# Three token scatters in two steps instead of two, and a smaller share of each step for the experts

## The chip, the cores and the metric

The kernel runs on one core of a Trainium2 chip. Its engines are TensorE (PE; weight loads are listed as PEld), VectorE (DVE), ScalarE (ACT), GpSimd (POOL) and SyncE (SP), each with its own instruction stream in program order; SP, ACT and POOL also issue DMAs. The metric is the device time of one execution in microseconds; lower is better.

## The reference, cut to what matters

The input is 8 sequences of 512 tokens with 256 features, all in float32. Two layers follow one another, each of the form x + attention(norm(x)) + feed-forward(norm(x)).

- Layer 0, attention: 16 heads of 16 features over all 512 tokens of a sequence, plain softmax.
- Layer 0, feed-forward: a mixture of 8 experts. Each token goes to the expert with the largest affinity. The expert normalizes the token again, applies a 256 to 1024 layer with ReLU and a 1024 to 256 layer, and the result is weighted by the sigmoid of the affinity.
- Layer 1, attention: causal attention, a convolution over three tokens whose output serves as queries of a second causal attention with the same keys and values, and an output projection.
- Layer 1, feed-forward: two low-rank products with a GELU between them.

```
assign = jnp.argmax(x @ centroids.T, axis=1)
h = relu(_layernorm(xs, ln_g[e], ln_b[e]) @ w1[e].T + b1[e])
ye = xs + h @ w2[e].T + b2[e]          # for the tokens of expert e
x = x + _L0_attn_ref(xn, ...) + _L0_ffn_ref(xn, ...)
```

## The kernel before, in words

Everything stays in SBUF but the tokens sorted by expert. The attention of layer 0 is cut into 32 jobs: 8 sequences, 4 groups of four heads. A loop of steps t = 0 to 268 (`run`, L442) does the attention; each job has 8 steps, and its scores are computed twice. First they are computed for the row maxima: PE at L345, DVE at L362 (`Job.scores`). A step 8 or more later, `Job.shift` (L375 to L382) transposes the maxima and writes them by four small SP DMAs into a spare row of the job's queries, so that the second computation (L394, `Job.exps`) gives scores already shifted; ACT takes their exponentials (L421) from step 12 on. `Job.attend` (L434) multiplies the exponentials with the values in every second step. When a job's last product is there, `l0_done` (L901) transposes and divides it on DVE (L904 to L908) and POOL adds it to the running sum `acc` (L912).

All other work of layer 0 is filled into these steps by the class `Work`. `fill(t, per_step, most)` (L118) runs after a step's scores and before its `attend`. It holds `room`, which grows by `per_step` = `MOE_PER_STEP` units a step, is capped at twice that, and falls by the cost of each piece placed. A piece is placed as long as room is above zero. Pieces with a due time (query, key and value projections at 1.75 units each, `shift` at 0.2) are forced when due and come first when due within four steps. Otherwise the next piece is drawn from one generator, `stream` (L843): a number is a cost, and `At(t)` closes the generator until step t. The order of instructions on every engine is the order in which these calls are made; no scheduler changes it.

`stream` runs as follows:

- The strings of `FIRST`, one per step: norms, transposes, affinities. In the second of them two SP DMAs fill the two DRAM buffers `hs_d` with zeros.
- `routing` (L673): the affinities of all tokens give each token its expert and its row in a buffer sorted by expert (`pos_i`), where each expert's rows are padded to blocks of 256 tokens, and each of the 23 blocks the row of its expert's weights (`wrow_i`). Then 32 scatters (L749), one for each 128 tokens: an indirect DMA from POOL writes 128 normalized tokens to their rows of one of the two `hs_d`, alternately, and `first_sum` (L609, POOL) adds the norm to `acc`.
- The memory of the norms is released, `load_ffn` issues weight loads on SP, and `Block(moe, 0)` is made: POOL gathers the 2.2 MB of the expert's weights `w` by an indirect DMA (L764), SP loads the block's 256 rows from both `hs_d` (L773), and POOL adds the two (L778). The generator then waits five steps.
- `banks_experts` (L218) gives the PSUM banks out anew: two banks for the maxima's scores and two for the exponentials' scores, where `banks_alone` (L211) gives three each; three banks instead of one for everything else.
- 23 expert blocks. Each has four `hidden` pieces (1.75 units: L807 on PE, ReLU on ACT L818 and DVE L820), `features` of the next block (0.5 units: transposes L785, `hsT` on DVE L790, which needs `w`), and two `output` pieces (3.5 units: L828, L837 and the store to `fs_d`, L839). The next `Block` is made after the first `hidden` piece.
- `banks_alone`, and the 26 strings of `SECOND`, one per step: POOL gathers expert results back (L512), DVE adds them (L522), and the norms, statistics and transposes for the first half of layer 1 follow.

Behind the loop come the feed-forward of layer 1 and its two attentions.

Of the kernel before, what the change touches and what calls it, by code (L numbers as in the profile page):

```python
# [37 lines left out]
STEPS = (8, 6)  # L38
LEAD = (12, 12)
EARLY = 4  # L40
MOE_PER_STEP = 2.08
LAG = 7


# [108 lines left out]
def block_kernel(ctx: ExitStack, tc: tile.TileContext, x, a0_wqk, a0_bqk, a0_wv, a0_bv, cent, experts,  # L153
# [412 lines left out]
    with ExitStack() as l0:  # L566
# [38 lines left out]
        def first_sum(b, c):  # L605

            norms, n = firsts0[b, c]
            a = acc[b][:, c, :]
            nc.gpsimd.tensor_scalar(a, a, norms.rs1[:, n : n + 1], norms.nm_t[:, n : n + 1], ALU.mult, ALU.add)  # L609
# [63 lines left out]
        def routing():  # L673
# [74 lines left out]
            for t in range(NT):  # L748
                nc.gpsimd.indirect_dma_start(  # L749
                    out=hs_d[t % 2][:, :],  # L750
                    out_offset=IndirectOffsetOnAxis(ap=pos_i[:, t : t + 1], axis=0),
                    in_=h0[t // NC][:, t % NC, :],
                    in_offset=None,
                )
                first_sum(t // NC, t % NC)
                yield At(todo.t + 1)

        class Block:

# [83 lines left out]
        def stream():  # L843
# [17 lines left out]
            for t, pieces in enumerate(FIRST):  # L861
                for p in pieces.split():
                    do[p[0]](int(p[1]))
                if t == 1:
                    for h in hs_z:
                        nc.sync.dma_start(out=h, in_=zeros.unsqueeze(1).to_broadcast([P, NBLK, 2 * D]))
                yield At(t + 1)
            yield from routing()
            later.close()
            moe = later.enter_context(tc.tile_pool(name="moe", bufs=2, reuse_waits="tile"))  # L870
# [28 lines left out]
        todo = Work()  # L899
# [54 lines left out]
        todo.stream = stream()  # L954
        run(jobs, todo, 0, MOE_PER_STEP, 99)
        later.close()
# [90 lines left out]
    for i in range(2):  # L1047
        t = l1.tile([P, 2, S + 2], F32, tag=f"ctxT{i}", name=f"ctxT{i}", bufs=1)
# [232 lines left out]
```

## Time and profile before

| | us |
|---|---|
| median of 3 runs | 2091.49 (2089.46 to 2093.51) |
| the profiled execution, its own time | 2091.93 |
| its span | 2090.0 |
| PE busy | 2001.5 (96%) |
| DVE busy | 1230.1 (59%) |
| ACT busy | 867.6 (42%) |
| POOL busy | 203.4 (10%) |
| L345, scores for the maxima, PE busy | 761.0 |
| L394, scores for the exponentials, PE busy | 681.2 |
| L807 and L828, experts, PE busy | 179.6 and 170.9 |
| L749, scatters, POOL busy | 33.0 (32 of 1.03 each) |
| granted PE clock, mean | 0.982 of full |

How to read it: times in the trace are microseconds from the start of the span. A busy PE is not PE at its peak, since ends of matmuls are modelled. A row of a timeline has start, length, engine, line, operation, output and inputs, the number of instructions merged, and in brackets how long the engine had stood idle and what ended that. A row of windows has the window, its length, the busy time of each engine with its number of instructions, the granted PE clock as a share of full speed, and DMA load.

### The profile page before, as it was taken

The page shows a single profiled execution, that of the slowest core. Times are in us where ns is not written, and L with a number is a line of the kernel's source. Part 1 is how long each engine was busy: PE and PEld are TensorE (multiplying, and loading weights), DVE is VectorE, ACT ScalarE, POOL GpSimd, SP SyncE. Part 2 cuts the span into 40 slices and gives each one's busy share as a digit, 9 for nine tenths or more (in the row PEclk, how much of TensorE's full clock was granted, in tenths as well). Part 3 has the DMA queues.
Part 4 walks back from the last instruction along what each step waited for, and adds up shares of the span by engine and source line. Part 5 has one row for each costly group of instructions (what it writes and reads, how often), then busy time and mean ns, then how long its engine had stood idle before and what let it go on. Part 6 is the DMA issues. An engine that isn't in the chain of part 4 may idle for free.

```text
span 2090.0 us, 35594 instructions
## 1 busy us (share of the span) xinstructions
PE 2001.5 (96%) x13672; PEld 1013.6 (48%) x13672; DVE 1230.1 (59%) x3565; ACT 867.6 (42%) x1690; POOL 203.4 (10%) x245
## 2 busy tenths in 40 slices
PE   5899999999999999998898999999999999999998
PEld 3334555555555555542334455554555555554554
DVE  5765555555455455565425666666666666666763
ACT  4444333333333333346541444444444444444444
POOL 4361010010110100013310000000000000000000
PEclk8899999999999999999997899999999999999999
DMA  9015132222322122202000000000000000000000
GB/s 329 25 64 184 59 117 81 94 79 96 117 78 97 67 108 107 74 26 80 21 0 1 2 2 2 2 12 2 2 13 2 12 2 12 2 12 2 2 12 21
DMA packets 46058, 105.60 MB, mean 51 GB/s; under 512 B 5953, under 2 KB 33985, under 8 KB 42945
## 3 DMA queue, kind: packets, MB, share of 16 engines
q0 software_dynamic: 6384, 59.78, 7.7%
q1 hardware_dynamic: 38656, 42.62, 6.1%
q8 instruction: 107, 1.75, 0.4%
q10 hardware_dynamic: 848, 0.93, 0.1%
q14 instruction: 63, 0.51, 0.1%
HBM read 76.05 MB, written 26.48 MB: 49 GB/s over the span
## 4 chain that ended last, share of the span: by engine, by line
PE 87%; DVE 6%; ACT 2%; issue 2%; DMA 1%; SPq 0%; POOL 0%; ACTq 0%; DVEq 0%; POOLq 0%
PE bank L345 30%; PE bank L434 13%; PE bank L828 8%; PE bank L807 8%; PE bank L293 5%; PE bank L412 4%; PE bank L1085 4%; PE bank L394 3%; PE bank L303 3%; PE bank L1103 2%; DVE m L362 2%; PE bank L990 1%; PE bank L1137 1%; PE bank L266 1%; PE bank L1003 1%
## 5 line engine op out<-in xcount | busy, mean ns | idle before, releaser
L421 ACT ACTIVATE e<-bank 128x512 f32<-128x512 f32 (+1 forms) x1280 | 639.1, 552 | 919.5 <-PE bank L394 460.4
L345 PE MATMUL bank<-k,q 32*128 32x512 f32 (+3 forms) x3072 | 761.0, 534 | 22.2 <-DVE m L362 18.3
L394 PE MATMUL bank<-q,k 32*128 32x512 f32 (+3 forms) x3072 | 681.2, 533 | 4.5 <-DMA q<-mT 3.4
L365 DVE CUSTOM_DVE_ANT_0 jk<-bank,cmask 128x512 bf16<-128x512 f32 (+3 forms) x1024 | 502.9, 491 | 240.8 <-PE bank L345 162.4
L345 PEld LDWEIGHTS bank<-k,q 32*128 32x128 f32 x3072 | 301.2, 186 | 384.1 <-issue 162.1
L362 DVE TENSOR_REDUCE m<-bank 128x1 f32<-128x512 f32 x512 | 328.9, 685 | 142.8 <-PE bank L394 111.8
L434 PE MATMUL bank<-e,v 128*32 128x512 f32 (+3 forms) x3072 | 317.4, 501 | 0.0
L394 PEld LDWEIGHTS bank<-q,k 32*128 32x128 f32 x3072 | 266.2, 186 | 15.0 <-issue 9.6
L807 PE MATMUL bank<-hsT,w 128*128 128x256 f32 x736 | 179.6, 389 | 1.3 <-DVE hsT L790 1.3
L828 PE MATMUL bank<-w,hT 128*128 128x256 f32 x736 | 170.9, 386 | 0.0
L807 PEld LDWEIGHTS bank<-hsT,w 128*128 128x128 f32 x736 | 133.3, 190 | 69.9 <-issue 52.8
L828 PEld LDWEIGHTS bank<-w,hT 128*128 128x128 f32 x736 | 137.4, 191 | 38.1 <-issue 21.0
L434 PEld LDWEIGHTS bank<-e,v 128*32 128x32 f32 x3072 | 67.5, 108 | 137.1 <-issue 132.0
L412 PE MATMUL bank<-mask_t,ident_bf 128*128 128x128 bf16 (+1 forms) x768 | 123.5, 244 | 0.0
L412 PEld LDWEIGHTS <-ident_bf 128*128 128x128 bf16 x768 | 44.0, 97 | 155.5 <-issue 140.5
L820 DVE TENSOR_SCALAR hT<-bank,w 128x256 f32<-128x256 f32 x92 | 44.5, 484 | 110.3 <-ACT hT L818 110.3
L1085 PE MATMUL bank<-ctxT,cw_sb 128*128 128x256 f32 x384 | 90.0, 383 | 2.1 <-DVE q L283 1.8
L365 DVE DVE_READ_ACCUMULATOR2_ANT m<- 128x1 f32 x1024 | 85.0, 83 | 0.0
L837 DVE TENSOR_TENSOR f<-bank,w 128x256 f32<-128x256 f32 x46 | 19.5, 425 | 104.2 <-PE bank L828 104.1
L285 ACT ACTIVATE k<-bank,bqk,rows 128x512 f32<-128x512 f32 x64 | 46.3, 773 | 73.8 <-PE bank L293 64.5
L818 ACT ACTIVATE hT<-bank,w 128x256 f32<-128x256 f32 x92 | 43.6, 474 | 79.8 <-PE bank L807 79.8
L1085 PEld LDWEIGHTS bank<-ctxT,cw_sb 128*128 128x128 f32 x384 | 70.1, 189 | 13.2 <-DVE q L283 3.2
(187 smaller groups left out, 1410.5 us busy)
## 6 DMA issues: line engine op xcount, KB each, us to landing
hs_d<-zeros SPq DMA_DIRECT2D x2, 5888.0 KB
hs<-hs_d SPq DMA_DIRECT2D x46, 256.0 KB
q<-mT SPq DMA_DIRECT2D x384, 2.0 KB
fs_d<-f SPq DMA_DIRECT2D x23, 256.0 KB
acc<-in_x SPq DMA_DIRECT2D x8, 512.0 KB
out<-acc SPq DMA_DIRECT2D x8, 512.0 KB
cw_sb<-in_conv_w SPq DMA_DIRECT2D x1, 768.0 KB
wqk<-in_a_wqk ACTq DMA_DIRECT2D x1, 512.0 KB
```

Of the source, the lines that this page charges most:

```text
L293: nc.tensor.matmul(ps, lhsT=w[:, k, col : col + P], rhs=src[:, k, :], start=(k == 0), stop=(k == 1))
L303: nc.tensor.matmul(ps[:, j * D : (j + 1) * D], lhsT=src[:, k, c * P : (c + 1) * P], rhs=w[:, k, :], start=(k == 0), stop=(k == 1),)
L345: lambda h=h, qc=qc, at=at, nk=nk: nc.tensor.matmul(heads[h % 2][:, at : at + nk], lhsT=self.q[h * PH : (h + 1) * PH, qc * P : (qc + 1) * ...
L362: nc.vector.tensor_reduce(self.m[:, qc, h, :], src, AX.X, ALU.max, negate=True)
L365: nc.vector.tensor_tensor_reduce(out=junk[:, :nk], in0=src, in1=cmask[:, S - nk :], scale=1.0, scalar=-3e38, op0=ALU.add, op1=ALU.max, acc ...
L394: lambda h=h, kc=kc, at=at, lo=lo: nc.tensor.matmul(heads[h % 2][:, at : at + S - lo], lhsT=self.k[h * PH : (h + 1) * PH, kc * P : (kc + 1 ...
L412: nc.tensor.matmul(heads[h][:, : len(blocks) * P], lhsT=ident_bf, rhs=mask_t[:, : len(blocks) * P], start=False, stop=True,)
L421: nc.scalar.activation(e[:, h, :], heads[h][:, :n], AF.Exp, scale=self.scale)
L434: nc.tensor.matmul(self.av[h * PH : (h + 1) * PH, lo:], lhsT=self.v[:, kc, 4 * self.g + h, :], rhs=es[h // 2][:, h % 2, :], start=first, s ...
L807: nc.tensor.matmul(ps[:, i * TB : (i + 1) * TB], lhsT=w[:, O_W1 + k * FF + fc * P : O_W1 + k * FF + (fc + 1) * P], rhs=self.hsT[:, k, :], ...
L828: nc.tensor.matmul(ps[:, 0:D], lhsT=self.hT[:, fc, j * P : (j + 1) * P], rhs=w[:, O_W2 + fc * D : O_W2 + (fc + 1) * D], start=(fc == 0), s ...
L1085: nc.tensor.matmul(ps[:, :w], lhsT=cw_sb[:, k, tap, c * P : (c + 1) * P], rhs=ctxT[b % 2][:, k, tap + lo : tap + lo + w], start=(k == 0 an ...
```

## The change

Two things are changed. The scatter loop of `routing` no longer closes the generator after each scatter: after the scatters t = 1, 4, 7, ..., 31 it goes on at once. Of 32 closings 11 go, so that steps take one, two, one, two, ... scatters and everything behind them in the generator comes eleven steps earlier in the program. `MOE_PER_STEP` falls from 2.08 to 1.97 units. The instructions themselves are the same, in another order.

```diff
@@ -38,7 +38,7 @@
-MOE_PER_STEP = 2.08
+MOE_PER_STEP = 1.97
@@ -753,7 +753,8 @@
                 first_sum(t // NC, t % NC)
-                yield At(todo.t + 1)
+                if t % 3 != 1:
+                    yield At(todo.t + 1)
```

## The prediction

> **What bounds the kernel now.** I read the page first: TensorE is busy nearly everywhere, so the change can only pay where PE has holes.
>
> ```profile
> PE 2001.5 (96%) x13672; PEld 1013.6 (48%) x13672; DVE 1230.1 (59%) x3565; ACT 867.6 (42%) x1690; POOL 203.4 (10%) x245
> ```
>
> Then I read ScalarE's timeline, because the first of a step's exponentials (L421) marks each step t of the layer-0 loop: two exponentials per step, the first pair belonging to t = 12. So step 40 starts at 146.25 us, step 51 at 173.45, step 244 at 931.25. The loop before the experts (steps 46 to 48 here) and among them (steps 81 to 84) looks like this:
>
> ```profile
> 163.42 1.08 ACT L421 ACTIVATE e<-bank 128x512 f32<-128x512 f32 x2 [1.35 <-PE bank L394]
> 165.52 1.09 ACT L421 ACTIVATE e<-bank 128x512 f32<-128x512 f32 x2 [1.02 <-PE bank L394]
> 167.38 1.08 ACT L421 ACTIVATE e<-bank 128x512 f32<-128x512 f32 x2 [0.78 <-PE bank L394]
> ...
> 295.48 1.09 ACT L421 ACTIVATE e<-bank 128x512 f32<-128x512 f32 x2 [4.63 <-PE bank L394]
> 300.21 1.08 ACT L421 ACTIVATE e<-bank 128x512 f32<-128x512 f32 x2 [3.65 <-PE bank L394]
> 302.67 1.09 ACT L421 ACTIVATE e<-bank 128x512 f32<-128x512 f32 x2 [1.37 <-PE bank L394]
> 305.70 0.60 ACT L421 ACTIVATE e<-bank 128x512 f32<-128x512 f32 x1 [0.66 <-PE bank L394]
> ```
>
> A step without filling takes 2.10 (even) or 1.86 us (odd) while three banks serve the scores; once banks_experts leaves two, it takes 2.46 (300.21 to 302.67). A step with filling is PE's sum: about 1.27 us odd, 2.26 even (with the eight attend matmuls), plus 1.73 us per 1.75 units. An empty odd step thus wastes 1.2 us of PE, an empty even one 0.2.
>
> Third, GpSimd's timeline: a scatter (L749) with its first_sum (L609) takes 1.79 us from start to start and nothing paces it in between but the attention sum of a finished job (L912), for which POOL stood idle 5.86, 6.12 and 6.12 us at steps 28, 36 and 44.
>
> ```profile
> 133.84 0.55 POOL L609 TENSOR_SCALAR acc<-acc,rs1e,nme 128x256 f32<-128x256 f32 x1
> 140.52 0.72 POOL L912 TENSOR_TENSOR acc<-acc,og 128x256 f32<-128x256 f32 x1 [6.12 <-DVE og L908]
> 141.39 1.03 POOL L749 DMA_INDIRECT hs_d<-h,pos_i  x1 [0.15 <-issue]
> 142.47 0.55 POOL L609 TENSOR_SCALAR acc<-acc,rs1e,nme 128x256 f32<-128x256 f32 x1
> 143.19 1.02 POOL L749 DMA_INDIRECT hs_d<-h,pos_i  x1 [0.17 <-issue]
> ...
> 162.52 1.03 POOL L749 DMA_INDIRECT hs_d<-h,pos_i  x1 [0.15 <-issue]
> ...
> 165.86 1.00 POOL L764 DMA_INDIRECT w<-in_experts,wrow_i  x1 [1.03 <-PE bank L394]
> 167.86 1.27 POOL L778 TENSOR_TENSOR hs<-hs,hs 128x512 f32<-128x512 f32 x1 [1.00 <-DMA hs<-hs_d]
> ```
>
> Last, PE at the first expert block: the last scatter starts at 162.52, the block's first matmul at 175.21, which is 12.69 us of scatter, weight gather (about 8.7 us to hsT) and transposes. PE lost only 1.27 us to it, in step 51.
>
> ```profile
> 173.28 0.66 PE L785 MATMUL bank<-ident,hs 128*128 128x128 f32 x4
> 175.21 1.10 PE L807 MATMUL bank<-hsT,w 128*128 128x256 f32 x4 [1.27 <-DVE hsT L790]
> ```
>
> **The change, part by part.** Every sum is against the profiled execution, 2091.93 us (span 2090.0); the median of the three runs is 0.44 us below it.
>
> *Where the steps fall.* The planner is a rule in the code and can be replayed. Scatters start at step 14 in both. Before, one per step: Block 0 is made at step 46, its features are in step 51 (the "+ 5"), the last expert piece in step 241, SECOND runs from 242 to 267 of 268. After: 1, 2, 1, 2, ... scatters per step, Block 0 at step 35, features at step 40, last expert piece in 243, SECOND from 244; its last piece f3 comes right behind the loop. The loop has 269 steps in both. So I compare the stretch from step 40 to step 244: before 931.25 - 146.25 = 785.0 us, the same 405.2 units of work in both.
>
> *Respreading (mostly a wash).* Steps by parity and units placed, with the median of their time before, and their number before (53 to 241) and after (42 to 243):
> even: nothing or 0.5, 2.46 us, 18 and 19; 1.75, 3.99, 46 and 50; 2.25, 4.43, 4 and 2; 3.5, 5.72, 19 and 20; 4.0, 6.11, 6 and 7; 5.25, 7.43, 1 and 3.
> odd: nothing or 0.5, 2.46, 14 and 22; 1.75, 3.00, 46 and 54; 2.25, 3.43, 3 and 0; 3.5, 4.73, 24 and 18; 4.0, 5.11, 8 and 7.
> Sums: 735.4 and 771.6, so +36.2. The rest of the stretch before: steps 40 to 52 took 39.5 us (with one projection pair on a single bank, step 43: 6.80 us) and 242, 243 took 4.1, together 43.6. After: steps 40 and 41 with 4.0 and 1.75 units, 6.11 + 3.00, plus 1.3 for the first hsT, 10.4. Gone: 33.2. Net +3.0. Then what lies over the medians: before 6.0 (1.4 for a wait on hs at step 179 over its class, near 679.3, 1.7 for a clock dip at step 190, 0.42 each time that a job's transposition lands in an empty odd step, three times; small rest). After: five such landings, 2.1, small rest 1.5, dips between 0 and 3.2, taken half: 5.2. Respreading: 3.0 - 0.8 = +2.2 us. The smaller share is what undoes the thirteen steps gained: empty odd steps grow from 14 to 22.
>
> *The scatters (the cost).* Emitting three per two steps gives POOL 12 scatters in eight steps, 12 x 1.79 + 0.87 for L912 = 22.3 us; eight such steps took 21.05 us (98.27 to 119.33, L912 to L912). So POOL, with its idle gone, becomes the pace. Scatter 3 starts at 90.84 as now; scatter 9 at 90.84 + 6 x 1.79 = 101.6; its sum and L912 end at 104.1; scatter 21 at 104.2 + 11 x 1.79 = 123.9; L912 ends at 126.4 (its input is there at 119.3, no wait); scatter 31 at 126.55 + 9 x 1.79 = 142.7 us. That is 19.8 us sooner than 162.52, while PE reaches the features 27.2 us sooner (146.25 against 173.45). The chain of 12.69 us then puts the first L807 at 155.4, 9.1 us into step 40 where it was 1.76 into step 51: a wait of 7.3 us more. PE is in order: behind the transposes stand step 40's hidden layers, its attend matmuls, and all of step 41, so exponentials and maxima wait too. Ends: the wait can be 4.5 if the weight gather starts as soon as POOL is free (1.03 us sooner) and the scatters keep 1.74, or 9.5 if further waits like the 1.76 us on a scatter's landing before 90.84 come in. I take 7.3, since every duration in it has a row.
>
> *What else moves with it.* SP: the ten loads of load_ffn and out_b (0.4 to 0.6 us each to issue) and Block 0's hs loads stand ahead of the next shift's row copies, as before; they now begin after step 33's shift, about 133, and are issued by 139, before the last scatter lands: hidden, worth at most 2 us if not. POOL: job 2's L912 (step 36) now stands behind the gather of w and the hs sum; its result has no reader before the experts end, and og's two buffers give 16 steps: nothing. Block 1's gather follows at about 150 and lands some 9 us later, its hs loads perhaps behind it, about 162; PE wants them in step 42, about 165: hidden by 2 to 3 us, and up to 3 us of new wait if that cover is gone.
>
> *The clock.* PE idles from 146.1 to 149 (hs sum) and from 150 to 155.4. What such holes do, in windows around the holes at 72.5 (3.39 us) and 961.9 (3.43 us); columns are window, its length, busy time of PE, PEld, DVE, ACT and POOL, clock:
>
> ```profile
> 71.10:74.50 3.40, 1.40 (x8) 0.33 (x2) 3.23 (x12) 1.08 (x2) 0.00 (x0) 1.00 0.00 0
> 77.90:81.30 3.40, 3.40 (x15) 0.90 (x12) 3.03 (x14) 2.19 (x4) 0.00 (x0) 0.50 0.00 0
> 81.30:84.70 3.40, 3.40 (x16) 1.28 (x9) 3.26 (x8) 0.09 (x1) 1.12 (x1) 0.50 0.01 2
> 965.40:968.80 3.40, 3.40 (x16) 0.61 (x16) 0.43 (x2) 1.51 (x3) 0.00 (x0) 0.50 0.85 269
> ```
>
> After the first hole PE worked 8.8 us at half speed, after the second 3.4. Hidden-layer matmuls are pure PE, so the loss is half of that: 1.7 to 4.4 us; I take 3.0, and 0 as the low end, since holes of 1.2 us left the clock at 1.00. The Trainium skill, "TensorE: Matmul & The Clock Gate", Part 1, says that after an idle window of about 3.4 us the clock halves and that one busy window restores it; by the rule alone the loss would be about 1.7 us and the sum 1.3 lower. The row at 77.9 to 84.7 shows two full busy windows still at half speed, so here the rule is too kind. It speaks against the change, as both do.
>
> *The end of layer 0.* SECOND two steps later, f3 behind the loop. Its norms and copies are ScalarE's: the last steps already run at 4.9 us a pair on four exponentials, four norms and a copy, the same instructions after. Against it, the last shift (mT at 961.58, queued behind eight statistics on DVE, PE idle 3.43 us for its rows) will stand behind only two. I take zero; ends -2.5 (that hole gone) and +2.5 (two norms 1.05, transposes 0.8, copy 0.6 exposed). Layer 1 is unchanged.
>
> **Sum:** +2.2 + 7.3 + 3.0 = +12.5; 2091.93 + 12.5 = 2104.4, and 0.44 less against the median: 2104 us.
>
> **Rivals.**
> *Block 0 is ready in time (not slower).* Place: L785 and L807 of block 0. If the scatters ran as fast as they are emitted, the last would start at step 35, 135.8 us, and the first L807 at 148.5, 2.2 us into step 40. Then only respreading remains, +2.2, and with the dips gone +0.6: about 2092 to 2094. It decides once the last scatter starts before about 137. For it: POOL's idle of 18 us. Against: the 1.79 us, constant in every burst.
> *The hole pulls more down.* The clock stayed at half for 20.5 us after 1139.5; that, or Block 1 late as well, adds 5 to 8 us: 2109 to 2112. Against: PE is full behind this hole, and was not there.
> *A gain after all.* The end of layer 0 gives back 2.5 and a clock dip, and the thin empty steps cost nearer 2.0 than 2.46 (30 x 0.46 = 14 us less): 2085 to 2088. Against: all 31 empty steps show 2.45 or more.
>
> **How the numbers follow.** Changes of 0.2% (4.2 us) are about what a measurement of this kernel can tell from none; its three runs spread over 4.1 us. Block 0 late, 2096 to 2108: 0.77. In time: 0.13. More pulled down: 0.06. Gain: 0.04. The low end of the late case, 4.5 + 0 + 0.6 = +5, less the runs' own 2 us, is 2095; the high end, 9.5 + 4.4 + 4 = +18, is 2110. Slower: the late case, the pulled down and a little of the in-time one, 0.85; same 0.11; faster 0.04.
>
> **What would show it.** In the changed profile: scatters at 1.79 us without idle before L912; the last one near 142.7; L785 waiting for POOL and L807 for hsT, together some 7 to 9 us idle on PE near 146 to 155; a clock of 0.50 after it; step 244 near 942; 22 empty odd steps at 2.46. I am wrong if L807 follows L785 within 2 us, if empty steps take 2.0, or if the end of layer 0 shortens by more than 3 us.

## The result and the profile after

The changed kernel is slower: 2103.86 us (median of 7 runs, 2096.19 to 2108.2) against 2089.46 (7 runs, 2088.76 to 2093.51), a ratio of 1.0064 with a 95% interval of 1.0049 to 1.0079. The forecast was 2104 us, slower. The profiled execution of the changed kernel took 2103.86 us, its span 2100.8; 10.8 us more than the span of before. Lines from L756 on stand one further down than before, so L807 is now L808.

TensorE is busy for 3 us more, in a span that is 11 us longer:

```profile
PE 2004.7 (95%) x13672; PEld 1013.6 (48%) x13672; DVE 1230.7 (59%) x3565; ACT 867.5 (41%) x1690; POOL 204.4 (10%) x245
```

GpSimd's timeline after the change. Scatters follow one another without a hole in front of L913, as the second line shows; the last one starts at 142.62 us (142.7 was forecast), and the first weight gather at 147.08.

```profile
122.90 0.55 POOL L609 TENSOR_SCALAR acc<-acc,rs1e,nme 128x256 f32<-128x256 f32 x1
123.42 0.71 POOL L913 TENSOR_TENSOR acc<-acc,og 128x256 f32<-128x256 f32 x1
124.29 1.03 POOL L749 DMA_INDIRECT hs_d<-h,pos_i  x1 [0.16 <-issue]
...
137.66 1.02 POOL L749 DMA_INDIRECT hs_d<-h,pos_i  x1 [0.96 <-DMA hs_d<-h,pos_i]
...
142.62 1.02 POOL L749 DMA_INDIRECT hs_d<-h,pos_i  x1 [0.97 <-DMA hs_d<-h,pos_i]
...
147.08 1.00 POOL L765 DMA_INDIRECT w<-in_experts,wrow_i  x1 [2.14 <-DMA hs_d<-h,pos_i]
```

TensorE's timeline at the first expert block: 3.24 us idle for POOL's sum of the token rows, 5.09 us for `hsT`. Before, it was 1.27 us in all.

```profile
150.39 1.11 PE L786 MATMUL bank<-ident,hs 128*128 128x128 f32 x4 [3.24 <-POOL hs L779]
156.59 5.63 PE L808 MATMUL bank<-hsT,w 128*128 128x256 f32 x16 [5.09 <-DVE hsT L791]
```

And `hsT` waits on VectorE for the weights:

```profile
155.94 0.99 DVE L791 TENSOR_SCALAR hsT<-bank,w 128x256 f32<-128x256 f32 x2 [8.08 <-DMA w<-in_experts,wrow_i]
```

ScalarE's timeline, whose exponentials (L421) mark the steps: step 40 starts at 147.21 and step 41 at 164.38. A step with the same 4.0 units takes 6.11 us elsewhere; this one takes 17.17.

```profile
147.21 1.08 ACT L421 ACTIVATE e<-bank 128x512 f32<-128x512 f32 x2 [0.78 <-PE bank L394]
160.38 0.47 ACT L819 ACTIVATE hT<-bank,w 128x256 f32<-128x256 f32 x1 [12.08 <-PE bank L808]
...
164.38 1.09 ACT L421 ACTIVATE e<-bank 128x512 f32<-128x512 f32 x2 [1.66 <-PE bank L394]
```

Windows over that hole (window, length, busy time of PE, PEld, DVE, ACT, POOL, granted clock, DMA share, GB/s): the clock is at 0.53 and 0.50 behind the first idle stretch.

```profile
146.00:150.00 4.00, 1.15 (x7) 0.31 (x6) 1.85 (x3) 1.52 (x3) 1.93 (x2) 1.00 0.57 140
150.00:154.00 4.00, 1.11 (x4) 0.71 (x4) 0.00 (x0) 0.00 (x0) 1.99 (x3) 0.53 0.96 401
154.00:158.00 4.00, 1.41 (x3) 1.18 (x4) 0.99 (x2) 0.00 (x0) 0.00 (x0) 0.50 0.96 403
158.00:162.00 4.00, 4.00 (x14) 3.16 (x12) 0.48 (x1) 0.47 (x1) 0.00 (x0) 0.69 0.91 369
```

By stage, in us between the first exponentials of the steps named. Two profiles of each kernel; the second ones are runs told of below.

| stage | before | before, again | after | after, again |
|---|---|---|---|---|
| start to step 40 | 146.3 | 146.6 | 147.2 | 145.2 |
| step 40 alone | 2.1 | 2.1 | 17.2 | 18.7 |
| steps 40 to 244 | 785.0 | 785.2 | 799.4 | 802.4 |
| steps 244 to 266, the end of layer 0 | 52.6 | 62.4 | 49.2 | 59.0 |
| step 266 to the end | 1106.1 | 1109.1 | 1105.0 | 1111.6 |

The loss is in steps 40 to 244: 14.4 us in the first pair, 17.2 in the second. The end of layer 0 varies by 10 us from one execution to another in both kernels, and is 3.4 us shorter after the change in both pairs.

### The profile page after: what moved, and what is told of

Its sections match the earlier page's. It is cut to its first block, busy times and chain, and to the rows that moved or that the text cites. A ratio compares the mean times of both kernels' runs of the same rounds, so it can differ in the third digit from the quotient of the medians.

```text
span 2100.8 us, 35592 instructions
## 1 busy us (share of the span) xinstructions
PE 2004.7 (95%) x13672; PEld 1013.6 (48%) x13672; DVE 1230.7 (59%) x3565; ACT 867.5 (41%) x1690; POOL 204.4 (10%) x245
## 4 chain that ended last, share of the span: by engine, by line
PE 85%; DVE 7%; ACT 3%; issue 2%; POOL 2%; DMA 1%; ACTq 0%; SPq 0%; DVEq 0%; POOLq 0%
PE bank L345 28%; PE bank L434 13%; PE bank L808 8%; PE bank L829 8%; PE bank L293 5%; PE bank L1086 4%; PE bank L412 4%; PE bank L394 3%; PE bank L303 2%; DVE m L362 2%; PE bank L1104 2%; PE bank L991 1%; PE bank L1138 1%; PE bank L266 1%; PE bank L1004 1%
## 5 line engine op out<-in xcount | busy, mean ns | idle before, releaser
L421 ACT ACTIVATE e<-bank 128x512 f32<-128x512 f32 (+1 forms) x1280 | 639.0, 552 | 933.9 <-PE bank L394 474.7
L808 PE MATMUL bank<-hsT,w 128*128 128x256 f32 x736 | 183.5, 394 | 5.1 <-DVE hsT L791 5.1
L808 PEld LDWEIGHTS bank<-hsT,w 128*128 128x128 f32 x736 | 135.2, 193 | 75.8 <-issue 60.3
```

Of the source, the lines that this page charges most:

```text
L421: nc.scalar.activation(e[:, h, :], heads[h][:, :n], AF.Exp, scale=self.scale)
L808: nc.tensor.matmul(ps[:, i * TB : (i + 1) * TB], lhsT=w[:, O_W1 + k * FF + fc * P : O_W1 + k * FF + (fc + 1) * P], rhs=self.hsT[:, k, :], ...
```

## The experiments

The theory on trial (A): POOL's scatters and the weight gather behind them arrive late, PE stands in step 40 and then runs cold. The rival (B): the smaller share and its empty steps are the whole loss. Each experiment is judged by its stages first, because the spread of single times, on one chip up to 14 us for the kernel before, is as large as what is sought.

**The scatters alone**

```diff
-MOE_PER_STEP = 1.97
+MOE_PER_STEP = 2.08
```

(against the changed kernel)

> The three scatters per two steps of the changed kernel with the old share of 2.08. By the planner's rule Block 0's features stay at step 40, the last expert piece comes in step 229 and SECOND runs from 230 to 255. Theory A (PE waits in step 40 for POOL's scatters and the weight gather, then runs at half clock): the wait of 8.3 us and the cold stretch stay, step 40 takes about 17 us. The steps from 40 to 256 cost some 3 us more by the table of steps, and the steps from 256 on, with no norms left in them, get shorter by up to 2.3 us a pair, six pairs: 2094 to 2104 us. Theory B (the smaller share and its empty steps are the loss, the wait is made up later): empty odd steps fall from 22 to 17, some 6 us, and the kernel comes near the one before, 2090 to 2098, with a short step 40 making no difference.

Measured: 2114.5 us, a ratio to before of 1.0081 (1.0051 to 1.0111). Both theories named a lower time; both missed. The wait is there, and its end lies where it did although PE came 3 us sooner (step 40 starts at 144.1), so POOL's chain sets it and not PE:

```profile
149.99 1.11 PE L786 MATMUL bank<-ident,hs 128*128 128x128 f32 x4 [5.91 <-POOL hs L779]
156.34 4.04 PE L808 MATMUL bank<-hsT,w 128*128 128x256 f32 x9 [5.23 <-DVE hsT L791]
```

What was mis-sized is the end. With the experts done at step 230, steps 230 to 256 took 85.4 us (909.4 to 994.8), 3.3 a step, against the 2.10 and 1.86 of unfilled steps before the experts, with the clock at half for 20.5 us in three stretches; the short pairs behind step 256 gave back 12.7 (13.1 us against 25.8 from step 256 to 266). Finishing the experts early bought nothing here.

**The share alone**

```diff
-MOE_PER_STEP = 2.08
+MOE_PER_STEP = 1.97
```

(against the kernel before)

> The smaller share, 1.97, alone; one scatter a step as before. By the rule Block 0's features are in step 51 as before, SECOND starts at 253, and its last ten strings come behind the loop. Theory A: no wait beyond the 1.3 us of before, no cold stretch, 39 empty steps against 32; the end is longer by norms without exponentials beside them but the pairs before it shorter: 2087 to 2095 us. Theory B (the share is the loss): most of the 14 us, 2098 to 2106.

Measured: 2109.91 us, 1.0066 (1.0045 to 1.0087). That is above both ranges; as a loss against before on this chip, 14.9 us, the number is B's, but the place is not. Step 266 starts 986.3 us into the span against 983.9 and 994.3 in the two profiles of before; what is lost stands behind it, 1126.1 us to the end against 1106.1 and 1109.1, where the last ten strings of SECOND now run with no attention beside them. The expectation had set them off against shorter pairs ahead of them; they cost 17 to 20 us. It also says why the share can only fall together with an earlier start.

**A scatter made cheaper for POOL**

```diff
-            nc.gpsimd.tensor_scalar(a, a, norms.rs1[:, n : n + 1], norms.nm_t[:, n : n + 1], ALU.mult, ALU.add)
+            nc.scalar.activation(a, a, AF.Identity, bias=norms.nm_t[:, n : n + 1], scale=norms.rs1[:, n : n + 1])
```

(in `first_sum`, against the changed kernel)

> The changed kernel with first_sum moved from POOL to ACT (same values, scale and bias of an Identity), so that a scatter takes POOL about 1.2 us instead of 1.79 and the order on PE is untouched. Theory A: the last scatter starts near 133 instead of 142.6, the first matmul of block 0 near 147 instead of 156.6, the wait in step 40 shrinks to at most 2 us and the clock stays up: 8 to 11 us gone, 2092 to 2096 us. Theory B (respreading is the loss): within 3 us of the changed kernel, 2101 to 2107. ACT takes 32 more instructions of some 0.53 us in steps where it is busy for half of the time.

Measured: 2105.18 us, 1.0051 (1.0033 to 1.0069). The time lies in B's range and not in A's, and the last scatter starts at 135.24 and not near 133. Step 40 fell from 17.2 to 13.9 us, not to some 8. GpSimd's timeline shows the reason: without the sum every other scatter stands idle for a landing (the two scatters after the first line below, 1.28 us and then 1.87 from start to start), so 32 of them still take 53 us. The scatters go to the two `hs_d` in turn, and each waits for the last but one, which wrote the same buffer. Behind the last scatter POOL stands idle for one of SP's loads (L876), and the gather starts 6.2 us behind that scatter instead of 4.5.

```profile
122.88 0.97 POOL L749 DMA_INDIRECT hs_d<-h,pos_i  x1 [0.92 <-DMA hs_d<-h,pos_i]
124.16 0.97 POOL L749 DMA_INDIRECT hs_d<-h,pos_i  x1 [0.30 <-issue]
126.03 0.97 POOL L749 DMA_INDIRECT hs_d<-h,pos_i  x1 [0.90 <-DMA hs_d<-h,pos_i]
...
135.24 0.97 POOL L749 DMA_INDIRECT hs_d<-h,pos_i  x1 [1.85 <-DMA hs_d<-h,pos_i]
139.01 0.75 POOL L876 TENSOR_TENSOR ob_sb<-ob_sb,fb_sb 128x256 f32<-128x256 f32 x1 [2.80 <-DMA fb_sb<-in_f_b]
141.48 0.98 POOL L765 DMA_INDIRECT w<-in_experts,wrow_i  x1 [1.73 <-PE bank L394]
```

So under POOL's 1.79 us lies a second floor, set by the landing and by having two buffers, about 1.6 us a scatter; a third buffer was not tried. The wait for the weights stays at 5.27 us, and the clock falls here too. The direction is A's, a shorter chain and a shorter step 40; steps 40 to 244 took 796.1 us, 3.3 less than in the first profile of the changed kernel.

**Ten steps ahead of the features**

```diff
-MOE_PER_STEP = 1.97
+MOE_PER_STEP = 2.0
-            yield At(todo.t + 5)
+            yield At(todo.t + 10)
```

(against the changed kernel)

> The changed kernel with ten steps instead of five between making Block 0 and its features (step 45), and a share of 2.00, so that SECOND starts at step 244 as in the changed kernel. Nothing moves off POOL. Theory A: step 45 starts near 157, when hsT can be ready, so the wait falls from 8.3 to 0 to 2 us and the clock stays up, while five more unfilled steps cost 10 us of which the experts' steps give back about the same: 2091 to 2096 us. Theory B: 2101 to 2107.

Measured: 2101.93 us, 1.0026 (1.0008 to 1.0043); that is in B's range for the time and not in A's, but the runs of before beside it had a median of 2095.01, so the time alone does not decide. By stage it is what A says: steps 40 to 244 take 786.2 us against 785.0 before and 799.4 after the change. TensorE's transposes wait for nothing, and ahead of its first expert matmul it stands idle for 1.68 us, while VectorE makes `hsT` (from 162.30 us, behind two row maxima); the weights are there by then. The step that holds the features takes 7.04 us, 1.9 over its class.

```profile
160.59 0.66 PE L786 MATMUL bank<-ident,hs 128*128 128x128 f32 x4
162.93 1.32 PE L808 MATMUL bank<-hsT,w 128*128 128x256 f32 x5 [1.68 <-issue]
```

The clock does not fall below 1.00 between 200 us and 930 us, nor around this block. The 13.2 us gained there are the wait, the cold stretch behind it and what the other spreading of the pieces (36 empty steps by the rule, against 41) gives. In this profile steps 244 to 266 took 61.5 us, the long form of the end; beside the second profile of before, which has that form too, its span is 2102.1 us against 2103.4.

**Both kernels once more**

> The changed kernel once more, unaltered, for a second profile beside e6. If the cost sits where theory A says, step 40 takes 17 us again and steps 40 to 244 799 us again, to a microsecond or two; what varies from execution to execution then lies behind step 244, where the steps are thin and the clock may fall. If step 40 to 244 varies by 5 us or more, the single profile was no witness. 2097 to 2108 us.

> The kernel before once more. Steps 40 to 244 take 785 us within 2 us; the stretch from step 244 to the last exponentials of layer 0, 52.6 us in the first profile, may be up to 10 us longer when the clock falls there. 2089 to 2100 us.

Measured, on one chip: the changed kernel 2112.91 us, above its range, 1.0056 (1.0035 to 1.0076); the kernel before 2096.0 us, 0.9974 (0.9957 to 0.999), against 2102.38 for the same kernel in the runs to which the four experiments of this chip are compared. Identical kernels differing by 0.26% with an interval that leaves out 1 says how far these times may be trusted on that chip. The stages are in the table above: steps 40 to 244 of before repeat within 0.2 us, those of after within 3.0, and step 40 took 18.7 us instead of 17.2.

**The hole kept warm**

```diff
             banks_experts()
+            warm(6)
-            nxt.features()
+            nxt.features(9)
...
-            def features(self):
+            def features(self, extra=0):
...
+                warm(extra)
                 self.hsT = self.moe.tile([P, 2, TB], F32, tag="hsT", name=f"hsT{n}", bufs=1)
...
+        def warm(n):
+            if n:
+                ps = bank()
+            for _ in range(n):
+                nc.tensor.matmul(ps, lhsT=ident, rhs=xT[NB - 1][:, 0, :], start=True, stop=True)
```

> The changed kernel with fifteen matmuls of 128 by 512 that nobody reads put into the hole of step 40: six ahead of Block 0's transposes (PE stood idle 3.2 us there), nine behind them (5.1 us). The wait for the weights stays. Theory A: the first expert matmul is still near 156.6, the clock stays at 1.00 behind it, and step 40 falls from 17.2 us to 14 to 15: 2.8 us less than the changed kernel, 2096 to 2105. If the cold clock cost nothing, step 40 stays at 17.

Measured: 2115.61 us, 1.0064 (1.004 to 1.0087), as slow as the changed kernel on that chip; neither the time nor step 40 came out as expected. The clock stayed up, as meant:

```profile
150.00:154.00 4.00, 4.00 (x13) 2.00 (x12) 0.00 (x0) 0.00 (x0) 1.39 (x2) 1.00 0.99 419
154.00:158.00 4.00, 4.00 (x10) 1.71 (x9) 0.99 (x2) 0.00 (x0) 0.00 (x0) 1.00 0.97 404
```

But the nine added matmuls ran 1.9 us past the moment at which `hsT` was ready (it starts on VectorE at 155.49, and in the changed kernel the matmul follows that start by 0.65, so 156.1; L815, the former L808, starts at 158.01), which gave the gain away, and step 40 took 19.8 us since PE reached it 3.2 us sooner. The cold clock can still be read: from the first expert matmul to step 41 it took 158.01 to 163.79 = 5.8 us here and 156.59 to 164.38 = 7.8 us in the changed kernel. Cold cost 2.0 us in that profile. The same stretch, with the same pieces, took 8.6 us in the second profile of the changed kernel and 7.4 in the halves with the early start below, so the cost lies between 1.6 and 2.8 us. As a remedy the experiment failed; as a measurement it did its work.

**Output pieces in two halves, in the kernel before**

```diff
-                for j in range(TB // P):
-                    blk.output(j)
-                    yield 3.5
+                for j in range(TB // P):
+                    for half in range(2):
+                        blk.output(j, half)
+                        yield 1.75
...
-        share_banks(mx=banks[:2], sc=banks[4:6], av=banks[6:7], mm=banks[2:4] + banks[7:])
+        share_banks(mx=banks[:2], sc=banks[4:6], av=banks[6:7], mm=banks[2:3] + banks[7:], out=banks[3:4])
```

Each half holds four of the piece's eight matmuls. The sum stays between the halves in a bank of its own, so that the other pieces share two banks instead of three; that part was not run alone.

> The kernel before (one scatter a step, share 2.08) with each output piece of 3.5 units given as two halves of 1.75, its sum kept in a bank of its own. By the rule SECOND still starts at 242, and only one of the experts' steps is left without work instead of 32. If an empty odd step wastes 1.2 us of PE and an empty even one 0.2, as the table of steps has it, steps 51 to 242 get shorter by 17 to 20 us: 2070 to 2078 us. If the empty steps only shift the work of VectorE and ScalarE and waste nothing, the time stays as before, 2089 to 2097, and respreading can't be what ate the gain of the earlier start.

> e8 unaltered, on the same chip as e9 and e10. 2074 to 2086 us; steps 40 to 244 763 us again.

Measured: 2083.13 us, 0.9907 (0.9883 to 0.9931), and on another chip 2067.38 us, 0.9889 (0.9861 to 0.9917). Faster than both kernels, though the first time is above its range of 2070 to 2078 and the second below its 2074 to 2086. Steps 40 to 244 take 763.5 and 763.4 us against 785.0: 21.5 us less with not one matmul removed, where the table of steps gives 20.2 for 31 empty steps fewer (17 even ones at 0.2 us and 14 odd ones at 1.2). ScalarE's timeline among the experts now has a filled step every time, 2.99 odd and 4.00 even, and no 2.46 between (compare 300.21 to 302.67 before):

```profile
298.15 1.08 ACT L421 ACTIVATE e<-bank 128x512 f32<-128x512 f32 x2 [2.90 <-PE bank L394]
...
301.14 1.08 ACT L421 ACTIVATE e<-bank 128x512 f32<-128x512 f32 x2 [0.66 <-PE bank L394]
...
305.14 1.08 ACT L421 ACTIVATE e<-bank 128x512 f32<-128x512 f32 x2 [1.66 <-PE bank L394]
...
308.13 1.08 ACT L421 ACTIVATE e<-bank 128x512 f32<-128x512 f32 x2 [0.66 <-PE bank L394]
```

So the price of an empty step is real, and nearly all empty steps here are made by a coarse piece: 3.5 units overdraw the room and leave the next step nothing.

**The halves with the early start**

The changed kernel with the halves; and the same with the wait of ten steps and a share of 2.0.

> The changed kernel with the output pieces halved as in e8. By the rule six of the experts' steps are left with nothing or half a unit instead of 41. If the respreading and the wait are two separate costs, step 40 still takes about 17 us and the steps behind it become full: 10 to 12 us more than e8, of which the end of layer 0 gives back 3: 2084 to 2094 us. If full steps also hid the wait, it would equal e8.

> e9 with ten steps instead of five ahead of Block 0's features and a share of 2.00: early start, no wait, hardly an empty step (five). If the early start is worth anything by itself, this beats e8. By the table of steps it doesn't: the same work, PE full in both, within 3 us of e8, 2074 to 2086 us.

Measured on the chip of the second run above: 2072.68 us, 0.9919 (0.9892 to 0.9947), and 2070.66 us, 0.9905 (0.9878 to 0.9931), beside 0.9889 for the halves alone. Steps 40 to 244: 771.1, 765.0 and 763.4 us. In the first, step 40 takes 17.14 us again; full steps behind it hide nothing of the wait. The first lies 7.7 us above the last there (5.3 in the medians), where 10 to 12 were expected in the stretch. All times of this chip are below the ranges expected. Without the wait the early start still does not pay: 1.6 us more in the stretch than the halves alone, 3.3 in the medians.

## Why the prediction was right, point by point

*Where the steps fall.* Right: step 40 holds the features, step 244 begins SECOND, and the classes of steps keep their times.

*The scatters.* Right in mechanism and nearly in size. POOL became the pace; the last scatter was off by 0.1 us. That is partly luck: the first scatter came 1.9 us sooner than in the profile of before, and three waits for landings among the last (0.96, 0.48, 0.97), which had been put into the high end only, took it back. They fall together with SP's ten loads (issued from 131.79 to 137.7 us), which the prediction had called hidden: a scatter took 2.5 to 2.7 us to land just ahead of them and 4.1 us at 133.28, with the share of the DMA engines at 0.69 and then 1.02 (132 to 136 and 136 to 140 us) against 0.18 to 0.23 before. No run moved the loads, so this is read from the traces and not shown by an experiment; the last scatter starts between 142.5 and 143.3 us in the second profile, with the old share and with the halves, too. The first expert matmul came at 156.59 instead of 155.4, because the gather started 4.5 us behind the last scatter and not 3.3. PE idled 8.3 us, within the 7 to 9 named; over before's 1.27 that is 7.1 against 7.3.

*The clock.* The window fell to 0.50 as forecast. The term was 3.0 us; set against the kept-warm run, the first profile of the changed kernel gives 2.0, and two others give 1.6 and 2.8. The changed kernel's clock stayed at half for 10.2 us (150.3 to 160.5), of which PE worked 1.1 us on the transposes, hidden under the wait for the weights, and the last 3.9 us on the experts; half of 3.9 is the 2.0. By the Trainium skill ("TensorE: Matmul & The Clock Gate", Part 1), one busy window of about 3.4 us at half clock, the estimate would have been 1.7.

*Respreading.* Right in sign, too small: some 4.6 us instead of 2.2. Steps 41 to 243 took 782.2 us against 779.8 in the sum (799.4 less 17.2; and 3.0 + 771.6 + 5.2). Of these 2.4 us, six landings of a job's transposition in an empty odd step instead of five make 0.4, and two waits of half a microsecond for the rows of `shift` (in steps 147 and 155, ended by DMA q<-mT) 1.0; a clock dip of 1.7 at step 174 is what the sum had taken for dips. The empty steps themselves kept their 2.46. How much of the loss is due to empty steps is told better by the halves: with hardly any empty step the change costs 7.7 us from step 40 to 244, with them 14.4; so, by one profile of each, 6.7 us are empty steps and 7.7 the wait with its clock, less what an early start saves.

*The end of layer 0.* Taken at zero with ends of -2.5 and +2.5; measured -3.4 in both pairs, outside the ends, and more than the 3 us that the prediction had named as a sign of being wrong. In the first pair the mechanism stood in the text as the low end: the last shift's DVE copy now stands behind two statistics instead of eight. TensorE's wait for the rows fell from 3.43 us to 1.37:

```profile
965.32 2.06 PE L394 MATMUL bank<-q,k 32*128 32x512 f32 x8 [3.43 <-DMA q<-mT]
```

before, and after

```profile
978.66 1.14 PE L394 MATMUL bank<-q,k 32*128 32x512 f32 x8 [1.37 <-DMA q<-mT]
```

The 2.06 us of the first line against the 1.14 of the second are the cold clock that followed the longer hole. In the second pair this wait is 1.91 us before and 3.82 after, so it can't be the cause there; those two profiles hold stops of different length (see the last section), and the cause of their 3.4 us stays open. A wait with a visible cause that the change moves should have been priced, not netted against a fear.

*The sum.* Forecast for the stretch and the end +12.5, measured +14.4 - 3.4 = +11.0, with +1.0 ahead of step 40 and -1.1 behind step 266 making the span's 10.8. Two errors, respreading and the end, nearly cancelled; that forecast and median agree within 0.2 us is luck, with seven runs that spread over 12.

*The rivals.* Block 0 in time: refuted, L808 came 6 us behind L786. The hole pulls more down: it did not; the clock rose after 10.2 us, and Block 1's rows, summed by 163.9 us, were there before step 42 began at 167.39. A gain after all: the end did give back 3.4 us, but every empty step still cost 2.46.

## What to carry to other kernels

A planner that places work by a budget can pay for coarse pieces: here each piece that overdrew the budget left a step in which the tensor engine waited for its partners, so cut the pieces to the budget before tuning the budget. Work started sooner is worth only the holes it fills; ask first which chain must deliver its inputs, how fast that chain can run once its slack is gone, and what stands behind the wait on an engine that takes its work in order. And judge a change of half a per cent by stages that repeat to a microsecond or three, not by totals that spread over ten.

## What the runs showed of the hardware that was not expected

A scatter from POOL to DRAM occupied POOL for 1.0 us and took 2.5 us to land. That landing set the pace in the run with the cheaper scatter, pairs of about 3.15 us, and it did so through the program: the scatter of 126.03 us started 3.15 us behind that of 122.88, which wrote the same buffer, while that of 124.16, by the same 2.5 us, had not yet landed. No limit of the chip itself on scatters in flight was measured.

In the second profile of before, PE, DVE and ACT all stand still for some 5 us at 939 to 944 us, while POOL goes on with its gathers; nothing of the program is late, and the trace names no cause ("remote", "issue").

```profile
938.80 0.60 ACT L421 ACTIVATE e<-bank 128x512 f32<-128x512 f32 x1 [0.82 <-PE bank L394]
...
943.84 1.42 DVE L362 TENSOR_REDUCE m<-bank 128x1 f32<-128x512 f32 x2 [5.22 <-remote]
...
944.59 1.21 PE L345 MATMUL bank<-k,q 32*128 32x512 f32 x1 [5.24 <-DVE m L362]
...
945.97 0.60 ACT L421 ACTIVATE e<-bank 128x512 f32<-128x512 f32 x1 [6.56 <-issue]
```

The clock then falls to half for 10.2 us, and the end of layer 0 takes 62.4 us instead of 52.6. The second profile of after and those of the cheaper scatter and of the ten steps have shorter stops like it between 942 and 958 us (TensorE idle 1.3 to 2.9 us, ScalarE 4.1 to 4.7); the first profiles of before and after do not. Of the profiles told of here, all with such a wait of 4 us or more in ScalarE or VectorE ("remote") have steps 244 to 266 at 58 us or more, and all without it at 54 or less. Its cause stays open; it is not the change, since the unchanged kernel has it in one execution and not in another.
